# Attention whose output projection reads undivided values, with the division in VectorE's addition, and seven of eight key blocks of the softmax sums on GpSimd

## The chip, the cores and the metric

The kernel runs on one core of a Trainium2 chip. The metric is the device time of one execution in microseconds; the time given for a kernel is the median of its runs. A core has five engines with instruction queues of their own: TensorE (PE in the profile, its weight loads PEld), VectorE (DVE), ScalarE (ACT), GpSimd (POOL) and SyncE (SP), which here issues the DMA transfers.

## What is computed

Input x is 4 sequences of 1024 tokens with 128 features. The block is a "macaron": half a mixture-of-experts feed-forward step, attention, and half a feed-forward step again, each on a layer norm of x and added to x. Cut to the attention, which the change touches:

```python
c_q, c_kv = h @ w_down_q.T, h @ w_down_kv.T          # latents of 64
q, k, v = heads(c_q @ w_up_q.T), heads(c_kv @ w_up_k.T), heads(c_kv @ w_up_v.T)   # 16 heads of 64
q, k = rope(q), rope(k)
scores = einsum('bhqd,bhkd->bhqk', q, k) / 8
attn = softmax(scores, axis=-1)
out = einsum('bhqk,bhkd->bhqd', attn, v)
out = out.transpose(0, 2, 1, 3).reshape(b, s, H * DH) @ w_out.T + residual
```

All of it is float32. The kernel doesn't form v: it multiplies the softmax weights with the latent c_kv (64 values per token), and with a matrix G per head pair that is the product of w_up_v and w_out. So one head's share of the output is (weights @ c_kv) @ G, and the division by the softmax sum can stand anywhere behind the exponentials.

## The kernel before

The program is one list of instructions whose order is written out by hand; no scheduler moves anything, and each engine works through its own part in order. There are three stages: the first feed-forward step, in which the rope of the first heads and the first maxima are already worked on; the attention; the second feed-forward step (`ffn2`).

The attention is cut into units. A unit U is 512 queries of one pair of heads (the two heads lie on the partition halves 0 to 63 and 64 to 127); there are 4 x 8 x 2 = 64. A unit has eight slots c0 to c7, one for each 128 keys, and two slots make a group, so a unit is four groups. I call them G0 to G3; the group number modulo 4 is their index. The main loop of `run` walks over groups. For each slot it issues:

- `passA` (L675 matmuls, L676 reduction): 128 queries against 512 keys of a unit 15 slots ahead, whose row maxima VectorE takes from the two banks of psA. When a unit's eight are done, `max_row` (L685, L687) turns the maxima into a row that a DMA puts into maxr.
- `score` (L703): for both heads three matmuls over the high and low parts of q and k and a fourth that takes the maximum off, into psS[0] and psS[1] in even slots, psS[2] and psS[3] in odd ones. ScalarE then takes the exponential into a tile p (L707).
- `accumulate` (L719): GpSimd adds the p tiles of a unit into acc. With DIRECT = 2 it adds the blocks c0 to c5, in five additions; c6 and c7 are left for `den`.

At the end of a group stand, in this order: the rope stages that are due (`rope(g, END)`), the functions put off to this group with `self.at` (`run_later`), a background step (`step(True)`), in G0 `den` of the unit before, and `values` (L726), which multiplies p of the two slots of the group before with the latent into psC; after slot c7 ScalarE copies psC to osb (L728).

`den` multiplies a column of ones with c6, c7 and acc (L738): twelve matmuls of 256 columns, four of them on four strips of 32 columns, summed in a bank from `aux`. ScalarE copies the sums (L740). One group later a DMA writes them to DRAM and another brings them back spread over 128 partitions of 8 (L745, L746). `invert` takes reciprocals (L754), writes them to DRAM (L757) and brings them back as a tile rB with a row per head, broadcast to 64 partitions each (L759). `outp` multiplies osb with rB on VectorE (L766); three groups later, in a G3, four matmuls of osb with G go to the bank psX (L771), and VectorE adds psX to x (L773).

The rope for one head group (`rope`): latents times up-projections into psX and psS[0] (L593), four products with cosine and sine on VectorE (L581), a difference and a sum on GpSimd (L600, L602), rounded copies on ScalarE (L607), and on GpSimd what the rounding left (L612, one instruction for each half), each stored by a DMA. The stages e and o are due at the end of G3, the copies and the remainders at the end of G0.

Layer norms, latents and routing of later stages are generators that `step` advances: one step in the middle of G0, G1 and G3 that may not use an auxiliary bank (`step(False)`), and one at the end of G2 and of G3 that may (`step(True)`).

Of the kernel before, what the change touches and what calls it, by code (L numbers as in the profile page):

```python
# [9 lines left out]
F32 = mybir.dt.float32  # L10
F32R = mybir.dt.float32r
AF = mybir.ActivationFunctionType
ALU = mybir.AluOpType
# [8 lines left out]
TPB = S // 128  # L22
# [4 lines left out]
AHEAD = 15  # L27
NSLOT = B * 128
NGRP = NSLOT // 2
DIRECT = 2  # L30
PBUFS = 7
NROPE = 9
ACTS = (4, 6, 7)
WLAG, GS, GD = 4, 17, 22
# [3 lines left out]
class Kernel:  # L38
# [530 lines left out]
    def rope(self, n, stage):  # L569


        nc, P = self.nc, self.prep
        w = self.rope_of.setdefault(n, {})
        b, m = divmod(n, 16)
        g, qk, h = m // 4, m // 2 % 2, m % 2
        scr = (self.k_scr if qk else self.q_scr)[b][g]
        cs = slice(512 * h, 512 * h + 512)

        def half(eo, k):
            w[eo, k] = P.tile([128, 512], F32, name=f"rt{eo}{k}", tag=f"t{2 * eo + k}")  # L580
            nc.vector.tensor_tensor(w[eo, k], w["ps"][eo], (self.cos, self.sin)[k][:, cs], ALU.mult)  # L581

        if stage == "fetch":
            assert (b, qk, h) in self.latents
            w["C"] = P.tile([128, 2, 512], F32R, name="C_l", bufs=2)
            self.dma(out=w["C"], in_=self.c_scr[b][h][:, qk])
        elif stage == "mm":
            ps = w["ps"] = self.rope_banks
            hi, lo = w["C"][:, 0, :], w["C"][:, 1, :]
            for k, (wt, c) in enumerate(((self.wup1, hi), (self.wup1, lo), (self.wup2, hi))):  # L590
                for eo in range(2):
                    r64 = slice(64 * eo, 64 * eo + 64)
                    nc.tensor.matmul(ps[eo], wt[r64, qk * 4 + g, :], c[r64, :], start=k == 0, stop=k == 2)  # L593
            half(1, 0)
            half(1, 1)
        elif stage in ("e0", "e1"):
            half(0, int(stage[1]))
        elif stage == "e":
            w["eo"] = P.tile([128, 2, 512], F32, name="eo", bufs=2)
            nc.gpsimd.tensor_tensor(w["eo"][:, 0, :], w[0, 0], w[1, 1], ALU.subtract)  # L600
        elif stage == "o":
            nc.gpsimd.tensor_tensor(w["eo"][:, 1, :], w[0, 1], w[1, 0], ALU.add)  # L602
        elif stage in ("hi0", "hi1"):
            k = int(stage[2])
            if k == 0:
                w["hi"] = P.tile([128, 2, 512], F32R, name="hi_r")
            nc.scalar.copy(w["hi"][:, k, :], w["eo"][:, k, :])  # L607
        elif stage == "dhi":
            self.dma(out=scr[0:2, :, :, cs].rearrange("s h i t -> (h i) s t"), in_=w["hi"])
        elif stage in ("lo0", "lo1"):  # L610
            eo = w["eo"][:, int(stage[2]), :]
            nc.gpsimd.tensor_tensor(eo.bitcast(F32R), eo, self.f(w["hi"][:, int(stage[2]), :]), ALU.subtract)  # L612
        elif stage == "dlo":
            self.dma(out=scr[2:4, :, :, cs].rearrange("s h i t -> (h i) s t"), in_=w["eo"])
            self.roped.add((b, g, qk, h))
            del self.rope_of[n]

    def attn_first(self):

        yield from self.attn_pre(0)  # L620
        steps = {-5: "fetch", 0: "mm e0 e1", 2: "e", 3: "o", 5: "hi0", 6: "hi1", 7: "dhi", 8: "lo0", 9: "lo1", 10: "dlo"}
        for t in range(-5, 6 * (NROPE - 1) + 11):
            yield
            for n in range(NROPE):
                for stage in steps.get(t - 6 * n, "").split():
                    self.rope(n, stage)
# [103 lines left out]
    def den(self, U):  # L730

        nc = self.nc
        osb = self.osb_of[U] = self.op3.tile([128, 512], F32, name="osb")
        pd = self.aux()
        parts = [self.p_of[8 * U + c] for c in range(8 - DIRECT, 8)] + [self.acc_of[U]]
        for k, part in enumerate(parts):
            for n in range(4):
                nc.tensor.matmul(pd[32 * n:32 * n + 32, 0:256], self.ones, part[:, n // 2, 256 * (n % 2):256 * (n % 2) + 256], start=k == 0, stop=k == DIRECT)  # L738
        dsb = self.op1.tile([128, 256], F32, name="dsb")
        nc.scalar.copy(dsb, pd[:, 0:256])  # L740
        dT = self.ms.tile([128, 8], F32, name="dT")

        def turn():
            d1 = self.dram.tile([4, 256], F32, name=f"d1_{U % 4}")
            nc.sync.dma_start(out=d1, in_=dsb[0:128:32, :])  # L745
            nc.sync.dma_start(out=dT, in_=d1.rearrange("h (p c) -> (h p) c", c=8))  # L746

        self.at(self.group + 1, turn)
        self.at(self.group + 2, lambda: self.invert(U, osb, dT))

    def invert(self, U, osb, dT):
        nc = self.nc
        rT = self.ms.tile([128, 8], F32, name="rT")
        nc.vector.reciprocal(rT, dT)  # L754
        rB = self.op2.tile([128, 512], F32, name="rB")
        d2 = self.dram.tile([2, 512], F32, name=f"d2_{U % 4}")
        nc.sync.dma_start(out=d2.rearrange("h (p c) -> (h p) c", c=8), in_=rT)  # L757
        for hh in range(2):
            nc.sync.dma_start(out=rB[64 * hh:64 * hh + 64, :], in_=d2[hh:hh + 1, :].to_broadcast([64, 512]))  # L759
        self.at(self.group + 2, lambda: self.outp(U, osb, rB))  # L760

    def outp(self, U, osb, rB):
        nc = self.nc
        P, half = divmod(U, 2)
        b, j = divmod(P, 8)
        nc.vector.tensor_tensor(osb, osb, rB, ALU.mult)  # L766

        def out():
            po = self.aux() if self.bankO is None else self.bankO
            for i in range(4):  # L770
                nc.tensor.matmul(po[:, i * 128:(i + 1) * 128], osb[:, i * 128:(i + 1) * 128], self.G[:, j, :], start=True, stop=True)  # L771
            xs = self.X[:, b * TPB + 4 * half:b * TPB + 4 * half + 4, :]
            nc.vector.tensor_tensor(xs, xs, po.rearrange("p (t d) -> p t d", t=4), ALU.add)  # L773

        self.at(self.group + 3, out)

    def run(self):
        nc, tc = self.nc, self.tc
# [69 lines left out]
            self.ffn(hp, fp, lambda blk: xs[blk % 4], self.wts, bg1, depth=3, acts=ACTS)  # L848

        self.attn_open(False, ring)  # L850
        self.op3 = ring.enter_context(tc.tile_pool(name="op", bufs=3))
        self.op2 = ring.enter_context(tc.tile_pool(name="op2", bufs=2))
        self.op1 = ring.enter_context(tc.tile_pool(name="op1", bufs=1))
        att = ExitStack()
        self.pp = att.enter_context(tc.tile_pool(name="pp", bufs=PBUFS))
# [13 lines left out]
        for _ in streams[2].pop() if streams[2] else ():  # L869
            pass  # L870
        assert not (streams[0] or streams[2])
        self.rest, self.rope_banks, self.bankO = self.psS[1:3], [self.psX, self.psS[0]], self.psX
        streams[2] += [self.attn_pre(b) for b in range(1, B)]
        turns = {"next": 0}
        needs = {}
# [19 lines left out]
                    return  # L895


        MID, END = {1: "e0"}, {-2: "fetch", 0: "mm", 1: "e1", 2: "e o", 3: "hi0 hi1 lo0 lo1", 4: "dhi", 5: "dlo"}

        def rope(g, table):  # L900
            for d, stages in table.items():
# [6 lines left out]
        for g in range(NGRP + 1):  # L908
            s0 = 2 * g
            self.group, self.slot = g, s0  # L910

            for s in range(s0, min(s0 + 2, NSLOT)):
                if s == s0 and s + AHEAD < NSLOT:
                    self.passA(s + AHEAD)
                for k in range(4):
                    for hh in range(2):
                        self.score(s, hh, k)
                if s == s0:
                    rope(g, MID)
                    if g % 4 != 2:  # L920
                        step(False)
                elif s + AHEAD < NSLOT:
                    self.passA(s + AHEAD)

            self.nrest = 0
            b, i = divmod(s0, 128)
            if i == 40 and 1 <= b < B:
                streams[1].append(pre2(b - 1))
            rope(g, END)
            self.run_later(g)  # L930
            if g % 4 >= 2:
                step(True)
            if g == 2:
                for n, fn in enumerate(self.loads(2)):
                    self.at(g + 1 + n // 4, fn)
            if g < NGRP and g % 8 == 7:
                P = g // 8
                if P + 3 < NP:
                    for n, fn in enumerate(self.loads(P + 3)):
                        self.at(g + 1 + n // 4, fn)  # L940
                if P == NP - 2:
                    self.ffn_weights2(self.QT[a], self.KT[a], self.QT[c])
                    self.dma(out=xs[0], in_=self.x2_scr[0])

            if g and g % 4 == 0:
                self.den(g // 4 - 1)
            for s in range(s0 - 2, s0):
                if s >= 0:
                    self.values(s)
# [78 lines left out]
```

## Time and profile before

| what | value |
|---|---|
| median of 3 runs (range) | 1803.73 us (1801.5 to 1804.94) |
| the profiled execution | 1803.11 us |
| its span, first to last instruction | 1801.3 us |
| mean granted TensorE clock | 0.989 |
| DMA | 129674 packets, 232.80 MB |
| share of 16 DMA engines taken by packets | 42.7% |
| the attention loop, about | 265 to 1640 us |
| in it, busy us: PE, DVE, ACT, POOL | 1357.5, 1031.7, 677.5, 1076.5 |

The span is some 1.8 us less than the execution's time; the rest lies ahead of the first and behind the last instruction. Rows of the profile read as line, engine, operation, written tile <- read tiles, shapes and count, then the busy time in us and the mean ns of one, then how long the engine was idle just before such instructions and what ended that. A float32 matmul leaves two records, one that uses the fast four-byte format leaves one; matmul durations overlap, so their pace is read from the starts. The chain of work gives for each piece its start, the us that it adds to the chain, and the engine, tile and line.

### The profile page before, as it was taken

How to read it: one execution, taken by the hardware profiler on the slowest of the kernel's cores; microseconds unless marked ns; L12 is line 12 of the kernel's file. 1: busy time of each engine (PE TensorE's matmuls, PEld its weight loads, DVE VectorE, ACT ScalarE, POOL GpSimd, SP SyncE). 2: the span in 40 equal slices, each digit the busy share in tenths (PEclk: the TensorE clock that was granted, in tenths of full speed). 3: DMA queues.
4: the chain of work that ended last, by engine and by line, in shares of the span. 5: the costliest groups of instructions: out<-in, count | busy, mean ns of one | idle time of the engine just before them, and what ended most of it. 6: DMA issues, size and time to landing. Idle time of an engine off the chain costs nothing.

```text
span 1801.3 us, 31304 instructions
## 1 busy us (share of the span) xinstructions
PE 1726.3 (96%) x11492; PEld 1030.3 (57%) x11492; DVE 1339.9 (74%) x1903; ACT 908.9 (50%) x1916; POOL 1339.3 (74%) x803
## 2 busy tenths in 40 slices
PE   7988889999999999999999999999999999999898
PEld 5777655555555555555555555555555555556676
DVE  6776658877777778777688777788777776835787
ACT  4666555444545445554444445454444444445454
POOL 4458678778887788877788777788888765556566
PEclk9999989999999999999999999999999999999899
DMA  6025445444444444454444544454444432124443
GB/s 196 1 71 170 135 129 165 145 145 147 130 142 142 150 145 130 130 153 142 141 135 136 160 140 131 143 142 147 136 144 140 130 95 72 31 96 129 129 124 100
DMA packets 129674, 232.80 MB, mean 129 GB/s; under 512 B 36336, under 2 KB 49776, under 8 KB 128880
## 3 DMA queue, kind: packets, MB, share of 16 engines
q1 hardware_dynamic: 129520, 230.80, 42.7%
q8 instruction: 90, 1.47, 0.4%
q14 instruction: 64, 0.52, 0.1%
HBM read 146.45 MB, written 84.02 MB: 128 GB/s over the span
## 4 chain that ended last, share of the span: by engine, by line
PE 78%; DVE 7%; ACT 7%; POOL 3%; issue 3%; DMA 1%; SPq 1%; ACTq 0%; POOLq 0%; DVEq 0%
PE psc L726 24%; PE ps_s L703 21%; PE ps_a L675 8%; PE ps_s L738 5%; ACT p L707 4%; PE psx L771 4%; PE ps_s L400 3%; PE ps_s L479 3%; PE psx L593 2%; DVE m L676 2%; PE psc L371 1%; PE psc L479 1%; PE psx L434 1%; PE ps_s L434 1%; ACT dtmp L383 1%
## 5 line engine op out<-in xcount | busy, mean ns | idle before, releaser
L676 DVE TENSOR_REDUCE m<-ps_a 128x2 f32<-128x1024 f32 x512 | 627.3, 1225 | 324.1 <-PE ps_a L675 323.9
L707 ACT ACTIVATE p<-ps_s 128x512 f32<-128x512 f32 x1024 | 531.0, 601 | 605.6 <-PE ps_s L703 605.4
L719 POOL TENSOR_TENSOR acc<-acc,p 128x1024 f32<-128x1024 f32 x256 | 609.7, 2382 | 43.0 <-ACT p L707 31.6
L726 PE MATMUL psc<-p,ckn 128*64 128x512 f32 x2048 | 496.2, 605 | 0.0
L703 PE MATMUL ps_s<-QT,KT 64*128 64x512 f32 x3072 | 447.3, 393 | 0.1
L719 POOL TENSOR_TENSOR acc<-p 128x1024 f32<-128x1024 f32 x64 | 152.2, 2377 | 251.4 <-ACT p L707 251.3
L703 PEld LDWEIGHTS ps_s<-QT,KT 64*128 64x128 f32 x3072 | 296.7, 185 | 60.2 <-issue 3.2
L726 PEld LDWEIGHTS psc<-p,ckn 128*64 128x64 f32 x2048 | 124.3, 136 | 213.7 <-issue 199.4
L675 PE MATMUL ps_a<-KT,QT 64*128 64x512 f32 x1024 | 234.6, 450 | 11.2 <-DVE m L676 11.0
L675 PEld LDWEIGHTS ps_a<-KT,QT 64*128 64x128 f32 x1024 | 98.5, 184 | 229.9 <-issue 83.8
L703 PE MATMUL ps_s<-maxr,one_row 64*128 64x512 f32 x1024 | 210.0, 392 | 1.0 <-DMA maxr<-mr 1.0
L612 POOL TENSOR_TENSOR eo<-eo,hi_r 128x512 fp32r<-128x512 f32 x128 | 185.0, 1463 | 0.0
L766 DVE TENSOR_TENSOR osb<-osb,rB 128x512 f32<-128x512 f32 x64 | 153.8, 2403 | 3.0 <-DMA rB<-d 3.0
L384 POOL TENSOR_TENSOR X<-X,dtmp 128x512 f32<-128x512 f32 x54 | 69.0, 1278 | 73.2 <-ACT dtmp L383 66.7
L703 PEld LDWEIGHTS ps_s<-maxr,one_row 64*128 64x128 f32 x1024 | 103.4, 185 | 23.0 <-DMA maxr<-mr 2.2
L487 POOL TENSOR_TENSOR p<-eo,p 128x512 fp32r<-128x512 f32 x42 | 62.6, 1496 | 42.0 <-ACT p L486 35.5
L602 POOL TENSOR_TENSOR eo<-rt,rt 128x512 f32<-128x512 f32 x64 | 81.8, 1279 | 0.0
L600 POOL TENSOR_TENSOR eo<-rt,rt 128x512 f32<-128x512 f32 x64 | 81.8, 1278 | 0.0
L607 ACT CAST hi_r<-eo 128x512 fp32r<-128x512 f32 x128 | 74.6, 640 | 6.9 <-DMA qs<-hi_r 3.6
L400 PE MATMUL ps_s<-xs,wg 128*128 128x512 f32 x192 | 66.6, 457 | 11.8 <-DVE p L408 10.7
L728 ACT COPY osb<-psc 128x512 f32<-128x512 f32 x64 | 37.6, 588 | 72.8 <-PE psc L726 72.8
L771 PEld LDWEIGHTS psx<-G,osb 128*128 128x128 f32 x496 | 60.8, 193 | 21.2 <-issue 21.2
(194 smaller groups left out, 2131.8 us busy)
## 6 DMA issues: line engine op xcount, KB each, us to landing
C_l<-cs SPq DMA_DIRECT2D x64, 512.0 KB
QT<-qs SPq DMA_DIRECT2D x256, 128.0 KB
KT<-ks SPq DMA_DIRECT2D x256, 128.0 KB
qs<-hi_r SPq DMA_DIRECT2D x32, 512.0 KB
qs<-eo SPq DMA_DIRECT2D x32, 512.0 KB
ks<-hi_r SPq DMA_DIRECT2D x32, 512.0 KB
ks<-eo SPq DMA_DIRECT2D x32, 512.0 KB
rB<-d SPq DMA_DIRECT2D x128, 128.0 KB
```

The costliest lines, as they stand in the source:

```text
L400: nc.tensor.matmul(p, w[:, a, e, :], xs[:, c, :], start=k == 0, stop=k == 2)
L600: nc.gpsimd.tensor_tensor(w["eo"][:, 0, :], w[0, 0], w[1, 1], ALU.subtract)
L612: nc.gpsimd.tensor_tensor(eo.bitcast(F32R), eo, self.f(w["hi"][:, int(stage[2]), :]), ALU.subtract)
L675: nc.tensor.matmul(self.psA[:, hh, :], self.QT[P % 3][r, 0, q0:q0 + 128], self.KT[P % 3][r, 0, kk * 512:kk * 512 + 512], start=True, stop= ...
L676: nc.vector.tensor_reduce(self.m_of[U][:, :, qb, kk], self.psA, AX.X, ALU.max)
L703: nc.tensor.matmul(ps, w, x, start=k == 0, stop=k == 3)
L707: nc.scalar.activation(self.p_of[s][:, hh, :], ps, AF.Exp, scale=0.125)
L719: nc.gpsimd.tensor_tensor(acc, self.p_of[s - 1] if c == 1 else acc, self.p_of[s], ALU.add)
L726: nc.tensor.matmul(self.psC[64 * hh:64 * hh + 64, :], self.ckn[b % 2][:, c, :], self.p_of[s][:, hh, :], start=c == 0, stop=c == 7)
L738: nc.tensor.matmul(pd[32 * n:32 * n + 32, 0:256], self.ones, part[:, n // 2, 256 * (n % 2):256 * (n % 2) + 256], start=k == 0, stop=k == D ...
L766: nc.vector.tensor_tensor(osb, osb, rB, ALU.mult)
L771: nc.tensor.matmul(po[:, i * 128:(i + 1) * 128], osb[:, i * 128:(i + 1) * 128], self.G[:, j, :], start=True, stop=True)
```

## The change

- DIRECT goes from 2 to 1: GpSimd adds seven blocks (c0 to c6, six additions), and `den` multiplies ones with c7 and acc only, eight matmuls in place of twelve. PBUFS, the number of p tiles, goes from 7 to 8.
- `den`'s second DMA brings the sums back another way: element by element, so that dT[p, 4 * head + i] is the sum of query 128 * i + p of that head. rB, d2 and their three transfers go, and so does the multiplication of osb.
- `outp` runs one group after the reciprocals, in a G3 of the same turn. The projection of each head is a matmul of its own over 64 partitions: head 0 into psX, head 1 into psS[0], eight matmuls. VectorE then adds each block of 128 queries to x with a multiplication by the reciprocal, four instructions a head: head 1 at once, head 0 in the middle of the next group (through the list `mid`). In the last stage the two banks of psA are used, and both are added at once.
- osb has two buffers in place of three.
- The two remainders of the rope ("lo0", "lo1") become one instruction of both halves.
- Background steps move: in the middle of G1 and G3, and at the end of G0, G2 (with an auxiliary bank) and G3 (without).

```diff
-DIRECT = 2
-PBUFS = 7
+DIRECT = 1
+PBUFS = 8
...
-        elif stage in ("lo0", "lo1"):
-            eo = w["eo"][:, int(stage[2]), :]
-            nc.gpsimd.tensor_tensor(eo.bitcast(F32R), eo, self.f(w["hi"][:, int(stage[2]), :]), ALU.subtract)
+        elif stage == "lo":
+            nc.gpsimd.tensor_tensor(w["eo"].bitcast(F32R), w["eo"], self.f(w["hi"]), ALU.subtract)
...
-            nc.sync.dma_start(out=dT, in_=d1.rearrange("h (p c) -> (h p) c", c=8))
+            nc.sync.dma_start(out=dT, in_=d1.rearrange("(h x) (y p) -> p (h x y)", x=2, p=128))
...
     def invert(self, U, osb, dT):
-        nc = self.nc
         rT = self.ms.tile([128, 8], F32, name="rT")
-        nc.vector.reciprocal(rT, dT)
-        rB = self.op2.tile([128, 512], F32, name="rB")
-        d2 = self.dram.tile([2, 512], F32, name=f"d2_{U % 4}")
-        nc.sync.dma_start(out=d2.rearrange("h (p c) -> (h p) c", c=8), in_=rT)
-        for hh in range(2):
-            nc.sync.dma_start(out=rB[64 * hh:64 * hh + 64, :], in_=d2[hh:hh + 1, :].to_broadcast([64, 512]))
-        self.at(self.group + 2, lambda: self.outp(U, osb, rB))
-
-    def outp(self, U, osb, rB):
+        self.nc.vector.reciprocal(rT, dT)
+        self.at(self.group + 1, lambda: self.outp(U, osb, rT))
+
+    def outp(self, U, osb, rT):
         nc = self.nc
         P, half = divmod(U, 2)
         b, j = divmod(P, 8)
-        nc.vector.tensor_tensor(osb, osb, rB, ALU.mult)
-
-        def out():
-            po = self.aux() if self.bankO is None else self.bankO
+        po = self.bankO or [self.psA[:, hh, :] for hh in range(2)]
+        for i in range(4):
+            for hh in range(2):
+                r = slice(64 * hh, 64 * hh + 64)
+                nc.tensor.matmul(po[hh][:, i * 128:(i + 1) * 128], osb[r, i * 128:(i + 1) * 128], self.G[r, j, :], start=True, stop=True)
+
+        def add(hh):
             for i in range(4):
-                nc.tensor.matmul(po[:, i * 128:(i + 1) * 128], osb[:, i * 128:(i + 1) * 128], self.G[:, j, :], start=True, stop=True)
-            xs = self.X[:, b * TPB + 4 * half:b * TPB + 4 * half + 4, :]
-            nc.vector.tensor_tensor(xs, xs, po.rearrange("p (t d) -> p t d", t=4), ALU.add)
-
-        self.at(self.group + 3, out)
+                x = self.X[:, b * TPB + 4 * half + i, :]
+                nc.vector.scalar_tensor_tensor(x, po[hh][:, i * 128:(i + 1) * 128], rT[:, 4 * hh + i:4 * hh + i + 1], x, ALU.mult, ALU.add)
+
+        add(1)
+        if self.bankO:
+            self.mid.append(lambda: add(0))
+        else:
+            add(0)
...
                 if s == s0:
                     rope(g, MID)
-                    if g % 4 != 2:
+                    if self.mid:
+                        self.mid.pop()()
+                    if g % 2:
                         step(False)
...
             self.run_later(g)
-            if g % 4 >= 2:
-                step(True)
+            if g % 4 != 1:
+                step(g % 4 != 3)
```

More of the change, by code (lines that the diff above doesn't have):

```diff
@@ L620, in attn_first @@
         yield from self.attn_pre(0)
-        steps = {-5: "fetch", 0: "mm e0 e1", 2: "e", 3: "o", 5: "hi0", 6: "hi1", 7: "dhi", 8: "lo0", 9: "lo1", 10: "dlo"}
+        steps = {-5: "fetch", 0: "mm e0 e1", 2: "e", 3: "o", 5: "hi0", 6: "hi1", 7: "dhi", 8: "lo", 10: "dlo"}
         for t in range(-5, 6 * (NROPE - 1) + 11):
@@ L732, in den @@
         nc = self.nc
-        osb = self.osb_of[U] = self.op3.tile([128, 512], F32, name="osb")
+        osb = self.osb_of[U] = self.op2.tile([128, 512], F32, name="osb")
         pd = self.aux()
@@ L850, in run @@
         self.attn_open(False, ring)
-        self.op3 = ring.enter_context(tc.tile_pool(name="op", bufs=3))
-        self.op2 = ring.enter_context(tc.tile_pool(name="op2", bufs=2))
+        self.op2 = ring.enter_context(tc.tile_pool(name="op", bufs=2))
         self.op1 = ring.enter_context(tc.tile_pool(name="op1", bufs=1))
@@ L871, in run @@
         assert not (streams[0] or streams[2])
-        self.rest, self.rope_banks, self.bankO = self.psS[1:3], [self.psX, self.psS[0]], self.psX
+        self.rest, self.rope_banks, self.bankO = self.psS[1:3], [self.psX, self.psS[0]], [self.psX, self.psS[0]]
+        self.mid = []
         streams[2] += [self.attn_pre(b) for b in range(1, B)]
@@ L895, in step @@
                     return
-        MID, END = {1: "e0"}, {-2: "fetch", 0: "mm", 1: "e1", 2: "e o", 3: "hi0 hi1 lo0 lo1", 4: "dhi", 5: "dlo"}
+        MID, END = {1: "e0"}, {-2: "fetch", 0: "mm", 1: "e1", 2: "e o", 3: "hi0 hi1 lo", 4: "dhi", 5: "dlo"}
         def rope(g, table):
@@ L923, in run @@
                     self.passA(s + AHEAD)
+            while self.mid:
+                self.mid.pop()()
             self.nrest = 0
```

## The prediction

> **What bounds the kernel now.** I read the engine totals first, then the chain of work that ended last, then one quiet turn of the attention loop in time order. A "turn" is one unit U: 512 queries of a head pair, eight key slots c0 to c7, four groups G0 to G3.
>
> ```profile
> PE 1726.3 (96%) x11492; PEld 1030.3 (57%) x11492; DVE 1339.9 (74%) x1903; ACT 908.9 (50%) x1916; POOL 1339.3 (74%) x803
> ...
> PE 78%; DVE 7%; ACT 7%; POOL 3%; issue 3%; DMA 1%; SPq 1%; ACTq 0%; POOLq 0%; DVEq 0%
> ```
>
> TensorE carries the chain. The chain inside a quiet turn, 1275 to 1298 us (start, us, what), shows how tightly:
>
> ```profile
> 1275.40 1.10 ACT p L707 x2
> 1276.50 0.04 issue
> 1276.54 1.50 PE ps_s L738 x24
> ...
> 1282.20 0.23 PE ps_a L675 x2
> 1282.43 0.23 PE psx L593
> ...
> 1291.88 0.23 PE ps_a L675 x2
> 1292.12 1.09 PE psx L771 x8
> 1293.21 1.87 PE psc L726 x8
> ...
> 1296.53 1.10 ACT p L707 x2
> 1297.63 0.04 issue
> 1297.67 1.48 PE ps_s L738 x21
> ```
>
> Everything left out is TensorE too. From one L738 to the next is 21.1 us; the only break is a short wait for an exponential before L738, which frees the bank that the sums go into. So a microsecond taken off TensorE in a turn is a microsecond off the turn, 64 times over, unless another engine comes up to it. The nearest is GpSimd, in the same turn (busy us: PE, PEld, DVE, ACT, POOL):
>
> ```profile
> 1275.00:1296.10 21.10, 21.03 (x155) 11.39 (x153) 15.89 (x18) 10.14 (x20) 17.28 (x9) 1.00 0.38 115
> ```
>
> The durations used below (count | busy us, mean ns | idle before):
>
> ```profile
> L719 POOL TENSOR_TENSOR acc<-acc,p 128x1024 f32<-128x1024 f32 x256 | 609.7, 2382 | 43.0 <-ACT p L707 31.6
> L612 POOL TENSOR_TENSOR eo<-eo,hi_r 128x512 fp32r<-128x512 f32 x128 | 185.0, 1463 | 0.0
> L766 DVE TENSOR_TENSOR osb<-osb,rB 128x512 f32<-128x512 f32 x64 | 153.8, 2403 | 3.0 <-DMA rB<-d 3.0
> L773 DVE TENSOR_TENSOR X<-X,psx 128x512 f32<-128x512 f32 x62 | 42.0, 677 | 14.0 <-PE psx L771 14.0
> L379 DVE SCALAR_TENSOR_TENSOR X<-psc,wts,X 128x128 f32<-128x128 f32 x40 | 11.2, 341 | 0.1
> ```
>
> **Denominator matmuls (TensorE, on the path).** L738 issues 24 records a turn (12 matmuls, two records each), four side by side in column strips: six rounds. The timeline gives starts 0.216 us apart, so six rounds are 1.30 us of the 1.43 to 1.50 in the chain and the rest is starting up. DIRECT from 2 to 1 drops two rounds: 0.43 us a turn, 64 x 0.43 = 27.6 us.
>
> **Output projection (TensorE, on the path).** Four matmuls over 128 rows (eight records, starts 0.111 us apart) become eight over 64 rows, in pairs on the two row halves: 16 records. What does a pair cost? The trace has fp32 pairs on half rows in setup:
>
> ```profile
> 41.07 1.09 PE L201 MATMUL ps_s<-wo,wv 64*64 64x128 f32 x16 [0.62 <-DVE xs L259]
> ...
> 814.46 1.16 PE L771 MATMUL psx<-G,osb 128*128 128x128 f32 x8
> ```
>
> Sixteen half-row records took 1.09 us there, eight full ones 1.16 here: pairs run together, a pair in about the time of one. L201's weights have 64 columns and the new ones 128; but 64-row, 128-column loads are in passA: its two loads start at 811.94 and the next pair's at 812.04, so two such loads take 0.10 us together. Eight pairs then stream for 8 x 0.111 = 0.89 us, as before. The 0.20 us that the chain's 1.09 has beyond 0.89 is the row against the rule. The Trainium skill (TensorEngine Tiling (Array Packing), Tiling Modes, Key Properties) says that changing the tiling mode drains TensorE. In the trace, passA (64 rows) is followed at once by the rope matmuls (64 rows: 1282.20 to 1282.43 and three bare 0.23 us), but the weight load of the full-array L771 has 0.37 us of issue idle ahead of it. Afterwards the projection has passA's mode, so one of two switches goes. By the row alone the step stays at 1.09 and saves nothing; by the rule it saves up to 0.20, 12.4 us over the 62 turns before the last stage. I take 0.15 us, 62 x 0.15 = 9 us.
>
> **GpSimd.** One more accumulation a turn: +2.38 us. The two "lo" subtractions of 1.46 us become one of 128x1024; between 2.38 (the same shape in L719) and 2.93 (twice the old): I take 2.4, as two of them took 2.54 us where L766 ran elsewhere (803.09) and 3.01 beside it (824.23), and L766 goes. A quiet turn goes from 17.3 to about 17.3 + 2.4 - 0.5 = 19.2 us, against a new turn of 21.1 - 0.6 = 20.5: 94%. It does not bound, but it loses nearly all its idle time. In the quiet turn c5's addition ends at 1292.7 with the exponential of c6 done at 1292.1; c6 is added until 1295.1, then the rope's e and o run until 1297.7. L738 reads the accumulator at about 1298.0: 2.9 us of cover. ScalarE's first hi copy reads e at 1298.46 (1297.84 in a shorter turn): 0.2 us. If that cover fails, the hi copies hold ScalarE, then the denominator's copy L740 is late, and behind it the bank of the next group's second score; another 1.4 us lies there. Single power operations (1.0 us) fit; steps with a power and an X addition (2.3 us), or the routing products (2 to 3 us), do not: nine to twelve events, 0 to 1 us each. I take +5 us (0 to 12).
>
> **VectorE.** Out go L766 (2.40 us, 0.68 when GpSimd is idle) and L773 (0.68); in come eight scalar_tensor_tensor. The row L379 has the same form: 11.2 / 40 = 0.28 us each, not stretched beside GpSimd, 2.24 us a turn. VectorE is relieved by 0.8 us. Its place matters more. Four run in G3's end behind passA's reduction (1292.16 + 1.23), so they end near 1293.4 + 1.2 = 1294.6 and free psS[0]. The next group's first score is at 1295.5; the four values matmul pairs and passA (1.87 + 0.42 us) are the cover, 0.9 us. If it is lost, the whole TensorE queue waits behind that score. The other four wait in G0 between two reductions 2.1 us apart, of which 0.9 us are idle: the second starts up to 0.3 us later, and its bank is wanted only after L738 and the values. Zero for both. The projection's second half also waits for psS[0] to be read by c6's first exponential (done by 1291.6, the projection starts at 1292.1): zero, unless ScalarE lags.
>
> **DMA and queues.** On SP's queue d2 and two rB transfers a turn go, and with them the wait for d2's landing (1289.72 to 1291.18) ahead of maxr, C_l and the QT/KT loads. Scores wait for maxr 3.2 us in all (1.0 + 2.2); I take -2. But dT is now gathered in 1024 elements of 4 bytes, not 128 of 32. The trace has no such transfer. The row: 128 packets start and end within 0.30 us, 0.94 us after the issue. By bytes, the cost stays 0.30. The Trainium skill (DMA: Bandwidth & Descriptors, Rules for kernel authors) speaks against the change: a non-contiguous last dimension becomes one descriptor per element. Then eight times the count costs 2.4 us. The reciprocal comes 6.8 us (median) after dT's issue, 5.5 after its last packet, so the rule leaves 3.4 us of cover and the row 5.5: zero in the loop. Behind the reciprocal on VectorE stand passA's reductions, and TensorE behind these. In the last turn the group is only some 2 us long and the wait is there already (6.6 us): +1 us (0 to 2).
>
> **Moved steps.** The background steps stay five a turn, two of them with permission for TensorE. One now runs before L738 and takes psS[1], which puts the sums into psS[2]; the step's own matmuls (0.4 to 0.9 us) cover that bank's later exponential. Buffers (8 p tiles, 2 osb tiles used for one turn) bind nowhere. Zero, between -2 and +3.
>
> **Sum** against the profiled execution, 1803.11 us (span 1801.3, 1.8 around it): -27.6 - 9 - 2 + 5 + 1 = -32.6, so 1770.5. The runs' median, 1803.73, stands 0.6 above that execution; I predict 1770.
>
> **Rivals.** (1) GpSimd catches up: its 94% in quiet turns is full in turns with background work, the hi copies are late in most of these, and a third to two thirds of the gain goes: 1803 - 13 = 1790 (1781 to 1800). For it: GpSimd already chains its additions without a gap in busy turns. Against: the 2.9 us at L738 and the quiet turns, about half. Chance 0.16. (2) Slower: the row halves do not run together with 128 columns. Place: L771's successor in G3. If the weight loads serialize, 16 x 0.111 = 1.78 us, +0.89, less 0.43: +0.46 x 62 = +28, so about 1830; it decides from 0.17 us a pair, where 8 x 0.06 eats the denominator's gain. Against it stand L201 and passA's loads. Chance 0.08. (3) dT's elements take over 7 us: the reciprocal stalls reductions in each turn, 1 us or more, 1840 and up. With 64 elements on each of 16 engines that is over 100 ns each, against 37 in the row (0.30 us for 8). Chance 0.06. (4) More than forecast: full switch saved, no GpSimd stall, reductions relieved: 1752. Chance 0.09. The forecast itself, 1758 to 1781: 0.61.
>
> **Chances.** Faster by over 0.2% (3.6 us, about what a measurement can tell from no change): 0.61 + 0.09 + most of (1) = 0.82; slower: (2) + (3) = 0.14; within: 0.04. The range leaves out (2), (3) and the far end of (4): 1755 to 1798.
>
> **What would show it.** L738 at 16 records and about 1.0 us in the chain; the projection at 16 records and 0.9 to 1.1 us; quiet turns of 20.5 us; POOL at about 19.2 us in them; no wait of the first score for VectorE, of the reciprocal for dT, or of L738 for acc. I am wrong if ACT hi_r waits for POOL eo in most turns, if the projection takes 1.8 us, or if the reciprocal's row shows DMA idle time in more than a few turns.

## The result and the profile after

| | before | after |
|---|---|---|
| median of 4 runs each (range) | 1804.34 us (1801.5 to 1805.81) | 1788.11 us (1787.77 to 1788.9) |
| ratio (95% interval) | | 0.9911 (0.9896 to 0.9926) |
| profiled execution, its span | 1803.11, 1801.3 us | 1788.01, 1786.2 us |
| first to last L738 (after: L737), 64 turns | 1367.2 us | 1352.6 us |
| behind the last one | 166.9 us | 169.2 us |

The kernel became faster by 16 us, where 34 were forecast. In the changed kernel the lines of the loop have moved by up to six; names of tiles stay. The engine totals (first row) and the shares of the chain of work, after:

```profile
PE 1690.4 (95%) x11492; PEld 1010.9 (57%) x11492; DVE 1318.9 (74%) x2287; ACT 906.9 (51%) x1916; POOL 1461.1 (82%) x803
...
PE 75%; DVE 12%; ACT 7%; POOL 3%; issue 3%; DMA 1%; SPq 0%; ACTq 0%; DVEq 0%; POOLq 0%
```

TensorE's busy time fell by 1726.3 - 1690.4 = 35.9 us; the forecast had taken 27.6 + 9 = 36.6 off it. But the span fell by only 15.1, so TensorE's idle time grew from 1801.3 - 1726.3 = 75.0 to 1786.2 - 1690.4 = 95.8 us, by 20.8. And VectorE's share of the chain went from 7% to 12%. Which waits grew? The waits of TensorE after (waiting tile and line <- engine, tile and line waited for: us in total, times, longest):

```profile
PE ps_a L674 <- DVE m L675: 18.4, 21, 2.1
PE ps_s L702 <- ACT dsb L739: 9.6, 8, 1.6
...
PE ps_s L702 <- DVE X L770: 2.5, 5, 0.5
PE ps_s L737 <- POOL acc L718: 2.5, 1, 2.5
```

Before, the first row was this, and there was none of the other three; a wait for maxr of 1.0 us is gone:

```profile
PE ps_a L675 <- DVE m L676: 11.0, 9, 2.1
```

So these waits grew by 7.4 + 9.6 + 2.5 + 2.5 - 1.0 = 21.0 us, about the idle time that is to be explained; other rows moved by less than 2 us each and nearly cancel. Not one of the four was in the forecast's sum at this size; m and X stood there at zero, and a late dsb only behind late hi copies.

A quiet turn has none of this. The same stretch as was shown of before, one turn from L737 to L737 (columns as there):

```profile
1290.05:1310.50 20.45, 20.39 (x151) 11.28 (x151) 14.60 (x24) 10.13 (x21) 19.07 (x10) 1.00 0.57 156
```

20.45 us against 20.5 forecast, POOL at 19.07 against 19.2. So the loss lies outside the quiet turns: in turns with a background step, and in the last turn, where the wait for acc stands. One of the first kind shows how. The chain of work there (start, us, what):

```profile
668.38 1.23 DVE m L675
...
670.98 2.38 DVE rstd L213
673.36 1.14 DVE m L675
...
674.55 0.50 PE ps_a L674 x2
...
676.66 2.76 PE psc L725 x8
```

and GpSimd in the same stretch, from the timeline (start, us, engine, line, operation and tiles, count, idle before):

```profile
668.50 7.26 POOL L718 TENSOR_TENSOR acc<-acc,p 128x1024 f32<-128x1024 f32 x3 [0.42 <-ACT p L706]
```

L213 adds a constant to 4 numbers per partition (a step of a layer norm). With no GpSimd addition beside it, it lasts 0.17 us; here it starts at 670.98, just as GpSimd's second addition of 7.26 / 3 = 2.42 us begins (668.50 + 2.42 = 670.92), and it ends with it, at 673.36. A reduction of the maxima stands behind it, and TensorE waits 2.04 us for that reduction. I call such an instruction "held". Over the loop such steps are found by their means. Of VectorE's groups with shapes kept apart, L222, the next step of the same layer norm (count, busy us, mean ns), before:

```profile
L222 DVE SCALAR_TENSOR_TENSOR rstd<-mv,rstd 128x4 f32<-128x4 f32 x11 | 10.1, 918 | 0.0
```

and after:

```profile
L222 DVE SCALAR_TENSOR_TENSOR rstd<-mv,rstd 128x4 f32<-128x4 f32 x11 | 18.0, 1636 | 0.0
```

The same 11 instructions take nearly twice as long; L213's 11 went from a mean of 685 to 1347 ns. All 34 instructions of the two lines in the loop went from 27.4 to 46.6 us in sum, though one group of six fell (L213 on rstdf, from 8.9 to 3.1 us). Of the 34 in after, 29 end 18 to 35 ns after a GpSimd addition or subtraction does. The other five take 0.17 us: four began with under 0.1 us of such an instruction left, one beside GpSimd's power L216. Instructions that read PSUM are not stretched: L770, the new additions, has a mean of 341 ns.

The new wait for dsb is a chain through three engines. At 683 us of after, from the timeline:

```profile
683.01 2.36 POOL L718 TENSOR_TENSOR acc<-p 128x1024 f32<-128x1024 f32 x1 [3.80 <-ACT p L706]
683.41 1.98 DVE L222 SCALAR_TENSOR_TENSOR rstd<-mv,rstd 128x4 f32<-128x4 f32 x1
...
685.42 0.88 ACT L227 ACTIVATE ya<-X,rstd 128x128 f32<-128x128 f32 x2 [1.48 <-DVE rstd L222]
686.21 0.35 ACT L739 COPY dsb<-ps_s 128x256 f32<-128x256 f32 x1
...
686.61 0.73 PE L702 MATMUL ps_s<-QT,KT 64*128 64x512 f32 x4 [1.01 <-ACT dsb L739]
```

L222 ends at 685.39, with the addition (685.37). ScalarE's normalisation L227 waits for it, the denominator's copy L739 stands behind L227 in ScalarE's order, and the next group's second score waits for the bank that L739 reads. In before no step stood at the end of G0, just ahead of `den`, and its trace has no such wait.

### The profile page after: what moved, and what is told of

Read it like the earlier page. It is cut to its first block, busy times and chain, and to the rows that moved or that the text cites. A ratio compares the mean times of both kernels' runs of the same rounds, so it can differ in the third digit from the quotient of the medians.

```text
span 1786.2 us, 31389 instructions
## 1 busy us (share of the span) xinstructions
PE 1690.4 (95%) x11492; PEld 1010.9 (57%) x11492; DVE 1318.9 (74%) x2287; ACT 906.9 (51%) x1916; POOL 1461.1 (82%) x803
## 4 chain that ended last, share of the span: by engine, by line
PE 75%; DVE 12%; ACT 7%; POOL 3%; issue 3%; DMA 1%; SPq 0%; ACTq 0%; DVEq 0%; POOLq 0%
PE psc L725 23%; PE ps_s L702 20%; PE ps_a L674 8%; ACT p L706 4%; PE ps_s L400 4%; DVE m L675 3%; PE ps_s L479 3%; PE ps_s L737 3%; PE psx L765 2%; PE psx L593 2%; POOL acc L718 2%; PE psc L371 2%; DVE X L770 1%; PE psc L479 1%; PE ps_s L434 1%
## 5 line engine op out<-in xcount | busy, mean ns | idle before, releaser
L718 POOL TENSOR_TENSOR acc<-acc,p 128x1024 f32<-128x1024 f32 x320 | 760.6, 2377 | 85.8 <-ACT p L706 68.0
L702 PEld LDWEIGHTS ps_s<-QT,KT 64*128 64x128 f32 x3072 | 292.7, 185 | 78.4 <-ACT dsb L739 13.5
L611 POOL TENSOR_TENSOR eo<-eo,hi_r 128x1024 fp32r<-128x1024 f32 x64 | 153.5, 2399 | 0.0
L770 DVE SCALAR_TENSOR_TENSOR X<-ps_s,rT,X 128x128 f32<-128x128 f32 x252 | 70.3, 341 | 17.4 <-PE ps_s L765 17.3
L400 PE MATMUL ps_s<-xs,wg 128*128 128x512 f32 x192 | 64.4, 444 | 10.5 <-DVE p L408 9.4
L770 DVE SCALAR_TENSOR_TENSOR X<-psx,rT,X 128x128 f32<-128x128 f32 x252 | 70.4, 342 | 0.0
L765 PEld LDWEIGHTS psx<-G,osb 64*128 64x128 f32 x504 | 66.1, 189 | 4.5
```

Source lines behind the costliest of these rows:

```text
L400: nc.tensor.matmul(p, w[:, a, e, :], xs[:, c, :], start=k == 0, stop=k == 2)
L611: nc.gpsimd.tensor_tensor(w["eo"].bitcast(F32R), w["eo"], self.f(w["hi"]), ALU.subtract)
L702: nc.tensor.matmul(ps, w, x, start=k == 0, stop=k == 3)
L718: nc.gpsimd.tensor_tensor(acc, self.p_of[s - 1] if c == 1 else acc, self.p_of[s], ALU.add)
L765: nc.tensor.matmul(po[hh][:, i * 128:(i + 1) * 128], osb[r, i * 128:(i + 1) * 128], self.G[r, j, :], start=True, stop=True)
L770: nc.vector.scalar_tensor_tensor(x, po[hh][:, i * 128:(i + 1) * 128], rT[:, 4 * hh + i:4 * hh + i + 1], x, ALU.mult, ALU.add)
```

## The theories and the experiments

Theory A: a held step. The seventh block fills GpSimd, so more of VectorE's small steps on SBUF meet an addition and last until it ends. Theory B: the new places of the background steps, above all the one ahead of `den` at the end of G0, cost the gain; GpSimd does not. Theory C, in the first set alone: GpSimd is full, and more work on it can only cost. Theory D, formed after the second set: the projection is worth less than was counted. Each kernel was timed in 5 rounds against before on the same chip. The three sets ran on three chips, with before's median at 1804.46, 1803.81 and 1804.15 us, so figures of different sets are compared as they stand. After's 1788.11 stands for after.

### First set: the layer norm's steps, the order of den, one block

`norm_after` and `norm_before` move L213 and L222, the layer norms' two small steps, from VectorE to GpSimd, beside the power that is there already; `norm_before` is the same edit on before.

```diff
-            nc.vector.tensor_scalar(rstd[:, :, 1], mv[:, :, 1], EPS, None, ALU.add)
...
-        self.nc.gpsimd.tensor_tensor(rstd[:, :, 0], rstd[:, :, 1], self.neghalf[:, :4], ALU.pow)
...
+        pool.tensor_scalar(rstd[:, :, 1], mv[:, :, 1], EPS, None, ALU.add)
+        pool.tensor_tensor(rstd[:, :, 0], rstd[:, :, 1], self.neghalf[:, :4], ALU.pow)
+        pool.tensor_tensor(rstd[:, :, 1], mv[:, :, 0], rstd[:, :, 0], ALU.mult)
+        pool.tensor_scalar(rstd[:, :, 1], rstd[:, :, 1], -1.0, None, ALU.mult)
...
-            nc.vector.scalar_tensor_tensor(rstd[:, :, 1], mv[:, :, 0], -1.0, rstd[:, :, 0], ALU.mult, ALU.mult)
```

> The changed kernel, with the three small VectorE steps of each layer norm (the epsilon, L213, and the shift, L222, both on SBUF alone) given to GpSimd, in four small operations where there was one. Theory A, held steps: these small operations wait on VectorE until GpSimd's running addition ends (2.0 to 2.4 us in place of 0.15), and everything behind them on VectorE and ScalarE is late; they stand ahead of all eight waits of the scores for dsb (9.6 us) and of some 9.7 of the 15.4 us that passA waits for the reductions. So 1788 - 9.6 - 9.7 - 1.7 (a half-clock spell after the longest) = 1767, within 5. Theory B, placement: it is the new places of the steps and of the additions to x on VectorE that make it late, whatever the small steps take: at most 4 us less, 1784 to 1788. Theory C, GpSimd is full: four operations in place of one make it slower, 1790 or more.

> The kernel before with the same move of the layer norms' small steps to GpSimd, as a control for norm_after. Theory A: in the kernel before all eight waits of passA for a reduction (9.6 us) have such a step ahead of them, and one half-clock spell (1.7 us) follows: 1804 - 11 = 1793, within 4; the difference between the two kernels then grows from 16 to about 26 us. Theory B: no difference, 1802 to 1806. Theory C: 1804 or a little more.

Measured: 1772.57 (1769.2 to 1777.69), ratio 0.9820 (0.9797 to 0.9843), and 1785.23 (1783.24 to 1786.91), 0.9888 (0.9870 to 0.9906). So moving the layer norm steps gives after 15.5 us, just short of A's range, but before 19.2 us, more than A said; in `norm_before`'s profiled execution 2.6 of 16.6 us lie outside the loop. B and C are wrong on both. The held steps cost time in both kernels; that they cost after more than before is not borne out, and A alone doesn't account for the shortfall.

`denfirst` calls `den` ahead of the step at the end of G0; `six` sets DIRECT back to 2, and is otherwise after.

```diff
+            if g and g % 4 == 0:
+                self.den(g // 4 - 1)
             if g % 4 != 1:
                 step(g % 4 != 3)
-            if g and g % 4 == 0:
-                self.den(g // 4 - 1)
```

> The changed kernel with the sums (den) ahead of the background step at the end of G0, so that ScalarE's copy of the sums no longer stands behind the step's normalizations. Theory A: the held shift L222 stays, but nothing that TensorE needs is behind it on ScalarE: the eight waits for dsb (9.6 us) go, the reductions' waits stay: 1778, within 3. Theory B gives the same here, if the moved step is all of the cause: more than 15 us less, 1773 or below. Theory C (GpSimd's late rope results hold ScalarE): the hi copies are still late, no gain, 1786 to 1789.

> The changed kernel with DIRECT back at 2: six key blocks on GpSimd, twelve matmuls for the sums; all else as changed. Quiet turns go from 20.45 to 20.88 us, which is 27.6 us in all. Theory A: GpSimd gets its gaps back and the loop's excess over quiet turns falls from 63 us towards the 38 of before: 1788 + 27.6 - 17 = 1799, from 1793 to 1804. Theory B: the excess stays: 1816, within 4. Theory C: as A.

Measured: `denfirst` 1780.88 (1776.88 to 1783.19), 0.9861 (0.984 to 0.9882), 7.2 us under after as A said, and the dsb row is gone from its waits, while the wait for m is still there (19.6 us in the loop, against 17.0). So of the 9.6 us of that row some 7 are time, and the wait for m takes up the rest. `six`: 1795.63 (1794.9 to 1797.71), 0.9947 (0.9929 to 0.9964). The seventh block, worth 27.6 us of matmuls, gives only 7.5 from six to after. A's range held, B's 1816 is wrong. `six` has a dsb wait as well (5.8 us), where before has none.

### Second set: the places of the steps, and the block alone

`oldsteps` puts the steps of after back where before has them; `newsteps_before` gives before the new places; `norm_oldsteps` joins `oldsteps` and the layer norm edit; `seven_before` is before with DIRECT = 1 (8 p tiles, and 2 osb tiles so that they fit).

```diff
-                    if g % 2:
+                    if g % 4 != 2:
                         step(False)
...
-            if g % 4 != 1:
-                step(g % 4 != 3)
+            if g % 4 >= 2:
+                step(True)
```

> The changed kernel with the background steps at their places of before: in the middle of G0, G1 and G3, at the end of G2 and G3 (both with an auxiliary bank). Theory B, placement: at the new places (end of G0 ahead of den; behind the additions to x) a step that waits for GpSimd meets work that TensorE needs; at the old ones it mostly doesn't. Nearly all of the 26 us lost in the loop come back: 1765, within 5. Theory A, GpSimd's density alone: the held steps are as long at the old places and as near to the reductions: 1783 to 1790. If each has a part, 1770 to 1780.

> The kernel before with only the background steps moved to the places of the changed kernel. Theory B: the loop loses what the run with six blocks lost against its own quiet turns, about 11 us: 1815, within 4. Theory A: nothing without the seventh block on GpSimd, 1804 within 4.

> The changed kernel with the layer norms' small steps on GpSimd and the background steps at their old places. Theory B: both costs go, the 26 us of the places and the held norms, which cost 19 us in the kernel before: 1746 to 1752, faster than every kernel so far. Theory A: only the norms count, and they were taken out already: 1768 to 1774.

> The kernel before with only DIRECT at 1 and eight p tiles (and two osb tiles, for room): seven blocks on GpSimd, eight matmuls for the sums, projection, division and steps as before. Quiet turns of 20.67 us are forecast, 27 us in all. Theory B: this comes almost whole, 1777 to 1781. Theory A: a denser GpSimd holds L766 and the small steps longer, and half of it goes again: 1788 to 1795.

| kernel | us (range) | ratio (interval) | against after |
|---|---|---|---|
| oldsteps | 1779.53 (1776.05 to 1781.82) | 0.9864 (0.9848 to 0.9880) | -8.6 |
| newsteps_before | 1846.65 (1845.66 to 1848.22) | 1.0238 (1.0224 to 1.0252) | |
| norm_oldsteps | 1760.65 (1758.88 to 1761.02) | 0.9759 (0.9746 to 0.9772) | -27.5 |
| seven_before | 1788.02 (1785.27 to 1793.74) | 0.9918 (0.9902 to 0.9934) | |

`oldsteps` gives back 8.6 us, about what `denfirst` did, and its dsb wait is 0.8 us: the new places cost after 7 to 9 us, by way of that copy. Neither A nor B has the whole of it. `newsteps_before` is 43 us slower than before, far more than either said. Its timeline shows one such wait; the multiplication L766, which the change removes, is the held instruction there, and L222 is behind it:

```profile
708.47 2.78 DVE L766 TENSOR_TENSOR osb<-osb,rB 128x512 f32<-128x512 f32 x1
...
711.18 1.22 DVE L222 SCALAR_TENSOR_TENSOR rstd<-mv,rstd 128x4 f32<-128x4 f32 x1
...
713.61 0.73 PE L703 MATMUL ps_s<-QT,KT 64*128 64x512 f32 x4 [2.25 <-ACT dsb L740]
```

An addition on GpSimd that begins at 708.34 is the one that L766 meets; ScalarE's normalisation and the copy of dsb follow L222 as in after. Eight waits for dsb make 15.5 us. Of the 43, TensorE's idle time has 24.0 (99.0 against 75.0) and its busy time 18.6 (1744.9 against 1726.3); six more spells of half clock than before has (last section) make about 10 of the second, and the rest was not traced.

`norm_oldsteps` is the fastest kernel of the study, 27.5 us below after and 43 below before, between the ranges of A and B. Its TensorE waits:

```profile
PE ps_a L675 <- DVE m L676: 4.8, 6, 1.4
PE ps_s L738 <- POOL acc L719: 4.3, 3, 2.5
...
PE ps_s L703 <- ACT dsb L740: 1.9, 7, 0.4
```

Against after, m falls by 13.6 us and dsb by 7.7; acc grows by 1.8. With the layer norm steps moved and the old places, the wait for GpSimd itself begins to show.

`seven_before`: 15.8 us from the block alone, where its matmuls would give 27.6. A's range held, at its lower end, and B's did not; but the mechanism that A names is not what its trace shows for the layer norm steps (see the account of the prediction).

### Third set: the projection alone, and GpSimd's instructions halved

`six_oldsteps` (after with DIRECT = 2 and the old places) differs from before by the projection with the form of dT, the joined remainder and the buffers alone. `norm_six_oldsteps` is the same with the layer norm edit. `six_split` is `six` with each addition in two halves, so that a held step would wait half as long, though GpSimd does slightly more. `norm_route_oldsteps` is `norm_oldsteps` with the small routing steps (all but reductions, reciprocals and one comparison) on GpSimd too.

```diff
-            nc.gpsimd.tensor_tensor(acc, self.p_of[s - 1] if c == 1 else acc, self.p_of[s], ALU.add)
+            for hh in range(2):
+                nc.gpsimd.tensor_tensor(acc[:, hh], (self.p_of[s - 1] if c == 1 else acc)[:, hh], self.p_of[s][:, hh], ALU.add)
```

> The changed kernel with six blocks on GpSimd (DIRECT 2) and the background steps at their old places: what is left of the change is the projection on undivided values, the division on VectorE and the joined lo. Quiet turns of 20.88 us against 21.10 of before, 14 us in all. Theory A (the seventh block makes GpSimd hold VectorE's small steps longer, and that is what is still lost at the old places, 17 us): nothing is lost here, 1790 within 4, so that the seventh block brings only 10 of its 27 us at the old places. Theory D, projection: the additions to x on VectorE (L770) delay the reductions and are what is still lost: 1797 to 1806.

> As six_oldsteps, with the layer norms' small steps on GpSimd. Theory A: 14 us under norm_before, 1771 within 4; the seventh block is then worth the 10 us to norm_oldsteps' 1760.65, as the routing steps are still held. Theory D: 1777 to 1785.

> The run with six blocks at the new places (six, 1795.6 us), with each GpSimd addition of 128x1024 issued as two of 128x512. GpSimd has 0.9 us more to do in a turn. If a held step waits for the end of the one running instruction, no hold is over 1.3 us in place of 2.4, and about half of some 16 us of waits goes: 1788 within 4. If it waits until GpSimd's queue has a gap, nothing is won, or something lost: 1795 to 1802.

> The kernel norm_oldsteps (1760.65 us) with the routing's small steps of the attention stage on GpSimd as well, but for the reductions, the reciprocals and the comparison L325, which it hasn't got. Theory A: the held routing steps stand ahead of 2.8 us of waits for reductions and 2.6 us for the additions to x; most of it goes: 1755 within 3. If GpSimd, 93% busy in quiet turns, can't take 3 us more in a batch's routing: 1760 or above.

| kernel | us (range) | ratio (interval) |
|---|---|---|
| six_oldsteps | 1795.46 (1793.26 to 1798.16) | 0.9952 (0.9937 to 0.9967) |
| norm_six_oldsteps | 1771.19 (1769.03 to 1773.36) | 0.9818 (0.9801 to 0.9835) |
| six_split | 1785.76 (1781.71 to 1787.09) | 0.9893 (0.9877 to 0.9909) |
| norm_route_oldsteps | 1772.20 (1771.36 to 1775.58) | 0.9826 (0.9809 to 0.9844) |

The projection gives 8.7 us by the first, less than A said and just more than D said. But with the layer norms out of the way (`norm_six_oldsteps` against `norm_before`, 1785.23) it gives 14.0, as A said, and about all that 0.22 us a turn can give over 63 turns. D falls; what the first lacks goes with the layer norm steps. `six` and `six_oldsteps` are equal within their intervals: with six blocks the new places cost nothing on balance. They trade waits: against `six_oldsteps`, `six` waits 5.9 us less for m (10.1 against 16.0) and 5.8 us for dsb, where the other doesn't wait.

`six_split` is 9.9 us faster than `six`, though its halves take more in sum than the whole (GpSimd busy 1348.7 against 1310.2 us). The held steps, in `six`:

```profile
L222 DVE SCALAR_TENSOR_TENSOR rstd<-mv,rstd 128x4 f32<-128x4 f32 x11 | 18.6, 1693 | 0.0
```

and in `six_split`:

```profile
L222 DVE SCALAR_TENSOR_TENSOR rstd<-mv,rstd 128x4 f32<-128x4 f32 x11 | 9.7, 884 | 0.6 <-POOL rstd L216 0.6
```

Shorter GpSimd instructions make VectorE's steps shorter, with no change to VectorE's program. That is what a step that waits for the end of the running GpSimd instruction would show, and not what a GpSimd short of time would. TensorE's waits for m and dsb fell by 3.5 and 4.2 us.

`norm_route_oldsteps` went the other way, 11.6 us slower than `norm_oldsteps`; A's 1755 was wrong. The wait for m is 14.0 us again, and one turn takes 29.5 us where `norm_oldsteps` takes 22.0. That GpSimd, already busy for 1483.5 us, is late itself with these steps is likely and not shown. This run says nothing on what held routing steps cost, since it put another wait in their place.

## Why the prediction was wrong

The time, 1788, is inside the range given, but the gain is less than half of the forecast. It stands where rival (1) put it, by luck: rival (1) named late hi copies in busy turns, and ScalarE's copies waited for GpSimd's results for 3.0 us in all. Two terms failed: that the moved steps cost nothing (8.6 us by `oldsteps`), and that the seventh block loses 5 us to a fuller GpSimd (12 to 20 in four pairs of kernels). The runs give two ways from before to after:

| way | projection | block | places | sum |
|---|---|---|---|---|
| block ahead of places | -8.7 (before to `six_oldsteps`) | -15.9 (`six_oldsteps` to `oldsteps`) | +8.6 (`oldsteps` to after) | -16.0 |
| places ahead of block | -8.7 (before to `six_oldsteps`) | -7.5 (`six` to after) | +0.2 (`six_oldsteps` to `six`) | -16.0 |
| forecast | -10 (-9, maxr -2, dT +1) | -22.6 (-27.6 and GpSimd's +5) | 0 | -32.6 |

The block and the places are not independent, so no single figure can be given to either. Step by step:

- **Denominator, -27.6.** Right as work: L737 has 16 records, and from its first start to the next instruction a turn takes 1.001 us against 1.433, 0.43 less, in 63 of the 64 turns. In the last turn it takes 3.87 us: with seven blocks the last addition has no cover, and TensorE waits 2.5 us for acc. All seven kernels with seven blocks have such a wait in the last turn, of 2.2 to 2.8 us, with a spell of half clock behind it, and none with six has either. The prediction looked for a last-turn cost at dT alone.
- **Projection, -9.** Right, and undersized. The lead of its first matmul behind passA went from 0.33 to 0.23 us and that of `values` behind it from 1.09 to 0.98: 0.20 us, all that the prediction had put down to a change of tiling mode, where 0.15 was taken. The Trainium skill (TensorEngine Tiling (Array Packing), Tiling Modes) says that such a change drains TensorE; the trace agrees, with these two leads. Pairs start 0.21 to 0.22 us apart only in stretches of half clock and about 0.111 elsewhere, so rival (2) is out. That TensorE's busy time fell as forecast to a microsecond is in part luck: 0.20 in place of 0.15 us a turn is 3 us more, and two more spells of half clock than before took about as much back.
- **maxr, -2.** Right in sign: the row (1.0 us) is gone.
- **dT.** Right: its reciprocal waits for it once, 7.3 us in the last turn, where before has 10.7 us in two waits. Rival (3) is out, though packets rose from 129674 to 167562.
- **Moved steps, "Zero, between -2 and +3".** Wrong with seven blocks: 7.2 us by `denfirst`, 8.6 by `oldsteps`, 11.9 with the layer norms moved (`norm_after` to `norm_oldsteps`). The prediction followed the banks and not ScalarE's order: the denominator's copy stands behind the normalisation of a step that is issued ahead of it. What a late copy does to the next score it had named, but for late hi copies alone.
- **GpSimd, +5 (0 to 12).** Wrong, in size and in kind. The seventh block's 27.6 us became 7.5 (`six` to after), 15.9 (`six_oldsteps` to `oldsteps`), 10.5 (both with the layer norms moved) and 15.8 (`seven_before`): the term was 12 to 20 us. The prediction looked for late hi copies and a late acc in the loop. In their place three things grew. The stretch behind the last L737 (L738) is 2.6 to 5.6 us longer in each of these four pairs, with the wait for acc and the half clock. TensorE's waits for m and dsb grew by 8.3 and 3.8 us from `six` to after, and by 2.2 and 0.8 from `six_oldsteps` to `oldsteps`. And the 33 small routing steps of the loop are held longer: 32.8 us in after against 27.3 in `six`, and 5 to 6 us more in the two other pairs that keep the layer norms on VectorE.
- **VectorE, zero.** The cover of 0.9 us for psS[0] was enough in all but five turns (2.5 us). What failed is the sentence that VectorE "is relieved": counted by busy time it was, but the steps that stand between two reductions were stretched by another engine. Before's own row for L766 had said it (2.40 us, "0.68 when GpSimd is idle"); I used it to credit the removal and didn't ask which other steps have the same form.

One reading that lies near is wrong: that the fuller GpSimd doubled the layer norm steps. The 34 of them take 45.4 us in `six`, with six blocks at the new places, and 46.6 in after; at the old places they take 33.0 in `six_oldsteps` and 33.9 in `oldsteps`, and 27.4 in before and 20.9 in `seven_before`. This is L222 in `seven_before`, where GpSimd is busy for 92% of the loop:

```profile
L222 DVE SCALAR_TENSOR_TENSOR rstd<-mv,rstd 128x4 f32<-128x4 f32 x11 | 9.8, 894 | 0.0
```

So their growth goes with the new places together with the new projection, and not with the seventh block. The places alone don't bring it: in `newsteps_before`, where L766 is held ahead of them, the 34 take 29.9 us. That the places decide which GpSimd addition a step meets, and how much of it is left, is likely and not shown by itself. The gains of the layer norm edit aren't larger with seven blocks either: 24.3 us from `six_oldsteps`, 18.9 from `oldsteps`, 19.2 from before, 15.5 from after.

What stays open: how the block's loss of 12 to 20 us divides among held routing steps, GpSimd's own lateness and the last turn. That a held step waits for the very end of the GpSimd instruction is read from coinciding ends and from `six_split`; what in the chip makes it wait, no run here shows.

## What to carry to other kernels

Ahead of filling an engine's idle time, list the short instructions of other engines that share something with it and whose consumers sit on the critical path; here GpSimd at 93% of a quiet turn was itself hardly late, but VectorE steps of 0.17 us took up to 2.4 us beside its additions. A background step that is moved must be followed through each engine's order: what is queued behind its last instruction there, and which bank does that free? And check a gain twice, as work (busy time of the bound engine) and as waits (its idle time by releaser): the first came out nearly as forecast here, and the second held the error.

## What the hardware showed that was not expected

- VectorE instructions that work on SBUF with two SBUF inputs, or as tensor_scalar in float32, of 0.15 to 0.2 us alone, took up to 2.4 us beside a GpSimd addition of 2.38 us; those reading PSUM, reductions, statistics and reciprocals did not. In the 14 traces 303 layer norm steps of 4 numbers began with over 0.25 us of a GpSimd instruction of 512 or more numbers left, and every one lasted to its end. Thirteen began like that beside GpSimd's power of 4 numbers (1.0 us), and none was held.
- GpSimd's additions kept their means (2.37 to 2.38 us in before and after). It isn't always spared: before's two L612 took 3.01 us where L766 ran beside them and 2.54 elsewhere.
- The clock can halve after a short wait, and doesn't always. Behind the 2.04 us wait at 674.5 the granted clock of a stretch of 3 us (third column from the right) is 0.59, and eight `values` records take 2.76 us of the chain, where a quiet turn has 1.87:

```profile
676.00:679.00 3.00, 3.00 (x16) 1.08 (x12) 1.44 (x5) 0.00 (x0) 3.00 (x3) 0.59 0.00 0
```

Behind a wait of 2.06 us that ended at 454.3 the clock stayed at 1.00 (456 to 459 us), and behind two of 1.38 and 0.53 us it fell to 0.50 (1225 to 1228 us); no run here shows what decides. Each such spell in the loop lasts 3.4 us and so costs about 1.7 us more than the wait ahead of it. Ahead of the last turn before has one, after two, `newsteps_before` seven (about 12 us) and `norm_oldsteps` none.
